# Placing TensorE's side work between attention steps: taking turns, early fetches, and an account of a small lead

## The chip, the cores and the metric

The kernel runs on one core of one Trainium2 chip. The metric is device microseconds (us) of one execution. Before the change it takes 8251.99 us, the median of three runs (8248.94 to 8252.69).

## The reference, cut to what matters

The input x has 4 images of 64 x 64 positions with 128 channels. Each image becomes 4096 tokens of 128 channels.

```python
# layer 0: two 3x3 convolutions, a gate, strictly causal attention with 4-wide queries and keys
c1 = conv_same(elu(x), W1, b1);  a, b = split(conv_same(c1, W2, b2), 2)
c3 = a * sigmoid(b)
q, k, v = c3 @ Wq + bq, c3 @ Wk + bk, c3 @ Wv + bv
x = x + c3 + tile(softmax_masked(q @ k.T / 4) @ v, 8) @ W3 + b3
# layer 1: full attention over 4096 tokens, 16 heads of 8, a gated FFN, 2 of 8 experts
n = layernorm(x)
h = n + concat_heads(softmax(q1 @ k1.T) @ v1) @ wo        # q1, k1, v1 = n @ wq, wk, wv
t = x + h + silu(h @ w1) * (h @ w3) @ w2
y = layernorm(t)
p, i = top_2(softmax(y @ router_w));  p = p / sum(p)
out = t + sum_j p_j * (y @ expert_w[i_j] + expert_b[i_j])
```

## The kernel before, in words

**The main work.** Layer 1's attention is 4096 *steps*: for each image (batch) b, each of 4 groups g of four heads, each of 8 blocks c of 512 queries and each of 32 tiles of 128 keys, one step (`attention_step`, L820) makes four score matmuls into two PSUM buffers `s` of 128 x 1024, two exponentials of 128 x 1024 on ScalarE into `e`, and four value matmuls that add into the one PSUM bank `acc`. There are three buffers `s` (L134), so the scores of a step and a half can stand ready. Layer 0's attention adds 36 such steps for each batch (`first_step`, L745), which put their sums in the bank `m`. In the main loop a step's values are issued after the scores of the second step after it (`finish(2)`, L1267).

**The side work.** Everything else that TensorE does (convolutions in Winograd form, projections, FFN, experts) is written as Python generators that are cut into *pieces*, each of about half a PSUM bank's worth of matmuls. All pieces share the one PSUM bank `m` (`bank`, L162; `m_tile`, L141): a *tile* here is one filling of that bank, made of a first piece, marked "held", and a last piece, marked "stop", and VectorE has to copy it out before the next tile may begin. A piece yields its estimated TensorE time (0.46 us for most, 0.0 for one that issues only VectorE, ScalarE, GpSimd or DMA work).

The generators are, for each batch: `convolutions` (L439), which turns the image into `c3`; `first_attention` (L576), which makes layer 0's queries, keys and values for a block and asks for its first steps; `second_operands` (L650), which makes layer 1's q, k and v of a block and writes them to device memory; and, for each block whose attention is complete, `last_part` (L863): attention output, FFN, router and experts. `last_part` starts by reading four operands from device memory, inverts the softmax sums on VectorE, writes them out and reads them back spread over the channels (`d_r<-sums`, `per<-d_r`).

**The order.** It is written out by hand: `InOrder` (L95) keeps each engine's instructions as the Python code issues them. `run_alone` (L1044) first brings batch 0 to the point where two blocks of second operands exist. Then the main loop (L1243) issues a step, and between the step's scores and an older step's values it may call `insert` (L245), which advances the first filler in the list `fillers` by one piece. It does so while `credit` is positive; `credit` grows each step by a rate that spreads the fillers' remaining estimated time (`PREPARE`, `LAST`, L1231) over the batch's remaining steps. No piece is inserted in a segment's first two steps (`quiet`, L1197). When the next segment's operands are not ready, the loop goes round without a step and inserts a piece each time (`waiting`): here called a *waiting place*.

`plan` (L1146) lets batch 0 begin with 2 blocks of keys (64 steps), go on when 4 exist (192 steps) and finish when all 8 do. Batch 0 thus computes its later blocks while its own attention runs. After `run_alone`, its chain is strictly sequential: `first_attention` calls the convolutions when it lacks `c3`, waits for its first steps, and then runs `second_operands` itself; `second_operands_beside` (L736) ends.

Of the kernel before, what the change touches and what calls it, by code (L numbers as in the profile page):

```python
# [12 lines left out]
ALU = mybir.AluOpType  # L13
# [102 lines left out]
def fast_path(ctx: ExitStack, tc: tile.TileContext, a: dict, where: dict, out: bass.AP, verdict):  # L116
# [122 lines left out]
    def advance(part):  # L239

        r = next(part[0], None)
        part[1] = max(0.5, part[1] - (r[0] if r else 0.0))
        return r

    def insert():  # L245
# [102 lines left out]
    def winograd(u, cols, v, bias, used, final):  # L348

        late = []  # L350
        for q, j in enumerate(COLS):
            sd = chunk("sd")
            s, d = wk.tile([P, QB // 2], FP, tag="sums", bufs=1, name="sums"), sd[:, : QB // 2]
            for pair in ((1, 2), (0, 3)):
                if late:
                    late.pop(0)()
                ps = bank()
                part = [ps[:, : QB // 2], ps[:, QB // 2 :]]
                for m, i in zip(part, pair):
                    product(m, u[:, 4 * i + j, cols], v[q][:, i])  # L360
                    if i == pair[0]:
                        yield 0.46, "held"
                if pair[0] == 1:
                    if alone[0]:
                        act.activation(sd, ps, AF.Copy)
                    else:
                        dve.tensor_copy(sd, ps)
                    dve.tensor_tensor(s, d, sd[:, QB // 2 :], ALU.add)
                    dve.tensor_tensor(d, d, sd[:, QB // 2 :], ALU.subtract)
                else:  # L370
                    t = chunk("neg", "t2")
                    if q == 0:

                        dve.scalar_tensor_tensor(t[:, : QB // 2], part[0], bias, s, ALU.add, ALU.add)
                        dve.scalar_tensor_tensor(t[:, QB // 2 :], d, bias, part[1], ALU.add, ALU.subtract)
                    else:
                        dve.tensor_tensor(t[:, : QB // 2], part[0], s, ALU.add)
                        dve.tensor_tensor(t[:, QB // 2 :], d, part[1], ALU.subtract)
                    used(q)
                    if q == 0:  # L380
                        one = t
                    elif q == 1:
                        both, less = chunk("pos", "both"), chunk("pos", "less")
                        (dve if alone[0] else pool).tensor_tensor(both, one, t, ALU.add)
                        pool.tensor_tensor(less, one, t, ALU.subtract)
                    elif q == 2:
                        late += final(0, t, both, ALU.add)
                    else:
                        late += final(1, less, t, ALU.subtract)
                yield 0.46, "stop"  # L390
        while late:
            yield 0.0, "stop"
            late.pop(0)()

    def first_band(st):

# [42 lines left out]
    def convolutions(b, st):  # L439
# [4 lines left out]
        def elu(n):  # L444

            todo = range(made[0], n)
            made[0] = max(made[0], n)
            neg, pos = {}, {}
            for at in range(len(todo) + 2 if todo else 0):
                a_, b_, c_ = (todo[i] if 0 <= i < len(todo) else None for i in (at, at - 1, at - 2))  # L450
                if b_ is not None:

                    pos[b_] = chunk("pos")
                    dve.tensor_scalar(pos[b_], xs[b_], 0.0, None, ALU.max)
                    dve.scalar_tensor_tensor(pos[b_], neg[b_], 1.0, pos[b_], ALU.min, ALU.add)
                    if b_ + 2 < NQ:
                        xs.append(load_x(b, b_ + 2, "xe"))
                if a_ is not None:
                    neg[a_] = chunk("neg")
                    act.activation(neg[a_], xs[a_], AF.Exp)  # L460
                if c_ is not None:
                    r, k = divmod(c_, 2)
                    ps = bank()
                    transposed(pos[c_], ps)
                    put = [(r, slice(1 + 8 * k, 9 + 8 * k), slice(0, 8))]
                    if k == 0 and r > 0:
                        put.append((r - 1, slice(17, 18), slice(0, 1)))
                    if k == 1 and r < 3:
                        put.append((r + 1, slice(0, 1), slice(7, 8)))
                    for band, to, of in put:  # L470
                        dve.tensor_scalar(
                            e_band[band % 2][:, to, 1 : IMG + 1], rows(ps)[:, of], -1.0, None, ALU.add
                        )
                yield (0.0 if c_ is None else 0.6), "stop"

        def first(r):
            band = c_band[r % 2]
# [50 lines left out]
        for n, (layer, r) in enumerate(jobs):  # L528
# [25 lines left out]
                if r == 3:  # L554
                    pool.memset(here[:, 17, :], 0.0)
            else:
                while alone[0] and len(st.ready) < 2 * r - 2:
# [18 lines left out]
    def first_attention(b, st):  # L576
# [3 lines left out]
        for c in range(NQ):  # L580
            while len(st.done) <= c:

                yield (0.0, "wait") if alone[0] else next(st.conv, (0.0, "stop"))
            while alone[0] and st.second < c - 1:
                yield 0.0, "wait"
            c3 = st.done[c]
            t = xt
# [46 lines left out]
            dve.tensor_tensor(t, ps, t, ALU.add)  # L634
            yield 0.6, "stop"

            while alone[0] and st.read < c:
                yield 0.0, "wait"
            sums, found = [], []
            for r in range(c + 1):  # L640
# [1 line left out]
            while not found:  # L642
                yield 0.0, "rounds"
            st.ready.append((t, found[0]))
            while not alone[0] and st.second <= c:
                yield from second_operands(b, st)
        dve.tensor_reduce(seen[:, 0, b : b + 1], top0.rearrange("p i c -> p (i c)"), AX.X, ALU.max)
        dve.tensor_reduce(seen[:, 1, b : b + 1], top_v0, AX.X, ALU.max)
# [1 line left out]
    def second_operands(b, st):  # L650
# [10 lines left out]
        for pair in range(2):  # L661
# [12 lines left out]
            yield 0.46, "stop"  # L674
        h = chunk("h")
        layernorm(t, h)
        for _ in range(2):
            yield 0.0, "stop"
# [57 lines left out]
    def second_operands_beside(b, st):  # L736

        while st.second < NQ:
            while len(st.ready) <= st.second or not folded[0]:
                if not alone[0]:  # L740
                    return
                yield 0.0, "wait"
            yield from second_operands(b, st)

# [75 lines left out]
    def attention_step(b, seg, kt, place, qx, vg, part):  # L820
# [19 lines left out]
        def values(es):  # L840
# [8 lines left out]
            if kt == seg.hi - 1:  # L849
# [5 lines left out]
                to = scratch[b]["a"][c, g] if seg.hi == NT else scratch[b]["p"][g, c]  # L855
                sp.dma_start(out=to, in_=at)
                if seg.hi == NT and g == NG1 - 1:
                    fillers.append([last_part(b, c), LAST])

        return scores, values  # L860


    def last_part(b, c):  # L863
        d = scratch[b]
        t, h, an = chunk("xt", "t"), chunk("xe", "h"), chunk("pos", "an")

# [4 lines left out]
        sp.dma_start(out=h, in_=d["h"][c])  # L871
        sp.dma_start(out=t, in_=d["t"][c])
        for _ in range(3):
            yield 0.0, "stop"
        dve.reciprocal(rs, rs)
        sp.dma_start(out=d["r"][c], in_=rs)
        per = chunk("pos", "per")
# [1 line left out]
            out=per, in_=d["r"][c].rearrange("(j i) n -> j (i n)", i=HD1).unsqueeze(1).to_broadcast([NH1, HD1, QB])  # L879
        )  # L880
        for _ in range(4):
            yield 0.0, "stop"
        dve.tensor_tensor(an, an, per, ALU.mult)
        yield 0.0, "stop"
        ps = bank()
        tokens(ps, an, wo1, range(2))
        yield 0.46, "held"
# [35 lines left out]
        dve.tensor_tensor(t, ps, t, ALU.add)  # L923
        y = chunk("h", "y2")
        layernorm(t, y)
        yield 0.46, "stop"
        for _ in range(3):
            yield 0.0, "stop"

        ps = bank()  # L930
        transposed(y, ps)
# [32 lines left out]
        yield 0.24, "stop"  # L964
        act.activation(pr, lg, AF.Exp)
        yield 0.0, "stop"
        yield 0.0, "stop"
        m1, w1 = top(pr, "a")
        rest = small("rest", [4, NE])
# [15 lines left out]
        by_block = d["g"][c].rearrange("(b e) (k a) -> b e k a", e=SLOT, a=SLOT)  # L985
        for b_ in range(4):
            sp.dma_start(out=g8.rearrange("e (k b a) -> b e k a", k=4, a=SLOT)[b_], in_=by_block[b_, :NE])
        for _ in range(6):
            yield 0.0, "stop"

        ps = bank()
        tokens(ps, g8, eb, range(2))
        yield 0.46, "held"
        tokens(ps, g8, eb, range(2, 4))
        dve.tensor_tensor(t, ps, t, ALU.add)
        yield 0.46, "stop"
        for k in range(4):
            tk = t[:, k * C : (k + 1) * C]
            by_e = wk.tile([P, NE, C], FP, tag="two", bufs=1, name="by_e")
            for half in range(2):  # L1000
# [8 lines left out]
                if half == 1:  # L1009
                    added = chunk("w", "added")[:, :C]  # L1010
                    dve.tensor_reduce(added, by_e.rearrange("p e c -> p c e"), AX.X, ALU.add)
                    dve.tensor_tensor(tk, tk, added, ALU.add)
                yield 0.46, "stop"
        sp.dma_start(out=tb_o[b][:, 4 * c : 4 * c + 4, :], in_=by_k(t))


# [23 lines left out]
            batches.append(self)  # L1040

    batches = []

    def run_alone(gens, until):  # L1044

# [182 lines left out]
        yield from spread(pool, taps2b, wino2[:, :, C:])  # L1228


    PREPARE, LAST = 149.0, 20.8  # L1231
    st = batches[0]
    left = run_alone(
        [st.conv, first_attention(0, st), second_operands_beside(0, st), fold_and_spread(), spread_beside()],
        lambda: st.second >= plan[0].n and len(spread_of) == 3,
    )
    alone[0] = False

    fillers.extend([gen, PREPARE] for gen in reversed(left[1:]) if gen is not st.conv)

    steps = stream()
    credit, waiting = 0.0, False
    while True:  # L1243
        if steps_in:
            do_step(steps_in.pop(0))
# [9 lines left out]
        b = now[0]  # L1255
        if batches[b].second == NQ and len(batches) == b + 1 and b + 1 < B:
            Batch(b + 1)
            fillers.append([first_attention(b + 1, batches[b + 1]), PREPARE])

        rate = 1.0  # L1260
        if batches[b].second == NQ:
            within = steps_left[b] - 40 if b + 1 < B else min(steps_left[b] - 40, 160)
            rate = sum(us for _, us in fillers) / max(1, within)
        credit = min(0.7, credit + rate)
        if waiting or credit > 0.0 and not quiet[0]:
            credit -= insert()
        finish(2)  # L1267
    finish(0)
    alone[0] = True
# [718 lines left out]
```

## Time and profile before

| | |
|---|---|
| median of 3 runs | 8251.99 us |
| the profiled execution's own time | 8255.66 us |
| its span | 8253.9 us |
| mean granted TensorE clock | 0.983 of full speed |
| TensorE busy | 8031.3 us, 97% |
| ScalarE busy | 7874.2 us, 95% |
| VectorE busy | 2468.4 us, 30% |
| GpSimd busy | 680.1 us, 8% |
| instructions of ScalarE | 8679, of which 8480 are exponentials |

The profile is of one execution, 3.7 us above the median. PE is TensorE, PEld its weight loads, ACT ScalarE, DVE VectorE, POOL GpSimd, SP the engine that issues the DMAs; "L105" stands on every row, because one helper issues every instruction, so rows are told apart by tile names. A TensorE that is shown busy may be computing at half clock, so its busy share says little by itself. ScalarE's records overlap: an exponential's record lasts 1.10 us on average, but the next one begins before it ends. In the view by stages each row is a stretch of time, with each engine's busy time in it, the granted clock and the DMA's share.

### The profile page before, as it was taken

Reading aid. Unit: us, or ns where it says so; the run is one execution under the profiler, and the core shown is the slowest. Engines: PE = TensorE matmul, PEld = TensorE weight load, DVE = VectorE, ACT = ScalarE, POOL = GpSimd, SP = SyncE. Lnnn points to the kernel's source line nnn. Section 1 sums busy time; section 2 is a strip of 40 time slices with the busy share of each in tenths; the row PEclk is TensorE's granted clock in tenths of the full one; section 3 lists DMA queues with packets and bytes.
Section 4 is the critical chain, followed back from the end, with each engine's and each line's share of the span. In section 5 each row is a group of like instructions: output and inputs, shape, how many; then the busy total and the mean of one; then the engine's idle time right before and its main releaser. Section 6 shows DMA issues by size and latency. Waiting matters only on the chain.

```text
span 8253.9 us, 172977 instructions
## 1 busy us (share of the span) xinstructions
PE 8031.3 (97%) x73299; PEld 2481.4 (30%) x73299; DVE 2468.4 (30%) x5068; ACT 7874.2 (95%) x8679; POOL 680.1 (8%) x615
## 2 busy tenths in 40 slices
PE   7799999999999999999999999999999999999997
PEld 3222222223333322333333333233333333332233
DVE  4433222222322223333322222343332222221223
ACT  3599999999999999999999999999999999999996
POOL 2210211000000003110000000311100000000000
PEclk8799999999999999999999999999999999999998
DMA  2121001101100001111100000111111111111211
GB/s 75 52 71 64 27 32 40 52 26 50 48 24 24 30 19 35 35 38 47 39 30 25 27 28 19 33 36 48 35 42 49 44 40 46 52 38 38 66 60 38
DMA packets 213940, 334.24 MB, mean 40 GB/s; under 512 B 31555, under 2 KB 107811, under 8 KB 213155
## 3 DMA queue, kind: packets, MB, share of 16 engines
q1 hardware_dynamic: 209139, 321.31, 11.9%
q8 instruction: 577, 9.45, 0.5%
q10 hardware_dynamic: 4016, 1.77, 0.1%
q14 instruction: 208, 1.70, 0.1%
HBM read 195.09 MB, written 127.93 MB: 39 GB/s over the span
## 4 chain that ended last, share of the span: by engine, by line
PE 87%; issue 7%; DVE 2%; ACT 1%; DMA 1%; POOL 1%; SPq 0%; ACTq 0%; DVEq 0%; POOLq 0%
PE acc L105 42%; PE s L105 29%; PE m L105 17%; ACT e L105 1%; DVE h L105 0%; POOL rs L105 0%; DMA f_kx<-d_k 0%; DVE pos L105 0%; DVE added L105 0%; DMA xe<-in_x_dram 0%; POOL xt L105 0%; DVE at L105 0%; SPq L105 0%; DMA d_r<-sums 0%; DVE two L105 0%
## 5 line engine op out<-in xcount | busy, mean ns | idle before, releaser
L105 ACT ACTIVATE e<-s 128x1024 f32<-128x1024 f32 (+1 forms) x8480 | 7814.2, 1101 | 144.5 <-PE s L105 137.9
L105 PE MATMUL acc<-e,vg 128*9 128x512 f32 x32768 | 4335.4, 595 | 1.0 <-DVE at L105 1.0
L105 PE MATMUL s<-qx,f_kx 32*128 32x512 f32 (+2 forms) x16960 | 2912.0, 496 | 40.3 <-ACT e L105 24.8
L105 PEld LDWEIGHTS s<-qx,f_kx 32*128 32x128 f32 (+1 forms) x16960 | 1165.5, 182 | 4089.1 <-ACT e L105 3872.2
L105 PEld LDWEIGHTS acc<-e,vg 128*9 128x9 f32 x32768 | 719.6, 90 | 798.0 <-issue 458.5
L105 PE MATMUL m<-v,f_wino 128*32 128x256 f32 x5744 | 468.1, 400 | 18.8 <-POOL v L105 7.3
L105 DVE TENSOR_TENSOR by_e<-m,gates 128x512 f32<-128x512 f32 x245 | 169.4, 691 | 681.6 <-PE m L105 681.6
L105 POOL TENSOR_TENSOR v<-r 128x1024 f32<-128x1024 f32 x120 | 232.6, 1945 | 1160.7 <-PE m L105 1160.3
L105 DVE COPY sd<-m 128x512 f32<-128x512 f32 x179 | 123.7, 691 | 633.5 <-PE m L105 633.5
L105 PE MATMUL m<-f_we,y2T 128*32 128x256 f32 x3920 | 313.1, 391 | 0.0
L105 POOL TENSOR_TENSOR rs<-ve,f_minus_half 128x4 f32<-128x4 f32 x64 | 65.3, 1020 | 2843.5 <-DVE ve L105 2819.8
L105 DVE TENSOR_REDUCE added<-by_e 128x128 f32<-128x1024 f32 x128 | 255.7, 1998 | 4.4
L105 DVE TENSOR_TENSOR t<-m,t 128x512 f32<-128x512 f32 x62 | 42.9, 692 | 698.7 <-PE m L105 698.7
L105 POOL TENSOR_TENSOR t<-t,h 128x512 f32<-128x512 f32 x32 | 40.9, 1277 | 2527.4 <-DVE h L105 2527.4
L105 DVE COPY at<-acc 128x512 f32<-128x512 f32 x130 | 89.9, 692 | 521.3 <-PE acc L105 521.3
L105 PE MATMUL m<-hT,f_fw 128*32 128x256 f32 (+1 forms) x2728 | 236.1, 391 | 0.0
L105 DVE TENSOR_TENSOR t<-m,sums 128x256 f32<-128x256 f32 x135 | 57.3, 424 | 480.1 <-PE m L105 480.1
L105 PEld LDWEIGHTS m<-v,f_wino 128*32 128x32 f32 x5744 | 116.4, 109 | 203.5 <-issue 155.0
L105 DVE SCALAR_TENSOR_TENSOR h<-m,h 128x512 f32<-128x512 f32 (+1 forms) x93 | 64.2, 690 | 352.6 <-ACT th L105 254.5
L105 DVE COPY h<-m 128x512 f32<-128x512 f32 (+1 forms) x93 | 64.2, 690 | 314.1 <-PE m L105 314.1
L105 PE MATMUL m<-e,f_v 128*32 128x512 f32 (+2 forms) x1128 | 154.0, 593 | 0.0
L105 DVE TENSOR_TENSOR e<-e,f_consts 128x128 f32<-128x128 f32 x128 | 29.1, 286 | 315.1 <-ACT e L105 315.1
(253 smaller groups left out, 3319.9 us busy)
## 6 DMA issues: line engine op xcount, KB each, us to landing
f_kx<-d_k SPq DMA_DIRECT2D x139, 512.0 KB
qx<-d_q SPq DMA_DIRECT2D x152, 256.0 KB
d_q<-two SPq DMA_DIRECT2D x64, 512.0 KB
d_a<-at SPq DMA_DIRECT2D x128, 256.0 KB
vg<-d_v SPq DMA_DIRECT2D x32, 576.0 KB
d_k<-two SPq DMA_DIRECT2D x32, 512.0 KB
d_v<-vc SPq DMA_DIRECT2D x32, 288.0 KB
xe<-in_x_dram SPq DMA_DIRECT2D x32, 256.0 KB
```

The lines of the kernel that those rows point to most:

```text
L105: made = op(*args, **kw)
```

## The change

The change touches the order of issue only; the matmuls, exponentials and transfers are the same, but for one zero-time piece.

1. **Turns.** What `run_alone` leaves of batch 0 (convolutions, first attention, second operands) becomes one filler, `together`, which goes round the three generators a piece at a time, finishing a tile once begun. Until four blocks of second operands exist (`plan[0].n + 2`), two pieces are inserted at a place in place of one. Tests of `alone[0]` inside the generators become tests of `b == 0`.
2. **Early fetch.** The first part of `last_part` (the reads, the reciprocal, `d_r`, `per`, the product) becomes `operands`, advanced by one part after each expert tile of the block before, if a later block is waiting. The product with the experts' bias (`tokens(ps, g8, eb)`) moves from before the experts to after them, and the six empty places that stood before it go.
3. **Account.** A piece is placed only when TensorE's lead, counted by four constants, covers it, or when credit is above 2.8. Places with no TensorE work, now marked "free", may be taken without credit. Credit may grow to 3.0 in place of 0.7; PREPARE is 143.3 in place of 149.0, LAST 18.9 in place of 20.8.

```diff
@@ advance @@
         part[1] = max(0.5, part[1] - (r[0] if r else 0.0))
+        part[3] = r is not None and r[1] in ("free", "rounds")
         return r
@@ first_attention @@
-                yield (0.0, "wait") if alone[0] else next(st.conv, (0.0, "stop"))
-            while alone[0] and st.second < c - 1:
+                r = (0.0, "wait") if b == 0 else next(st.conv)
+                if r[1] != "done":
+                    yield r
+            while b == 0 and st.second < c - 1:
                 yield 0.0, "wait"
...
-            while not alone[0] and st.second <= c:
+            while b > 0 and st.second <= c:
                 yield from second_operands(b, st)
@@ second_operands_beside @@
-                if not alone[0]:
-                    return
                 yield 0.0, "wait"
@@ last_part, its head split off @@
+    def fetch(b, c):
+        if (b, c) not in fetching:
+            fetching[b, c] = operands(b, c)
+        return next(fetching[b, c], fetching) is None
+
+    def fetch_following(b, c):
+        keys = [part[2] for part in fillers]
+        at = keys.index((b, c)) + 1
+        if at < len(keys) and keys[at]:
+            fetch(*keys[at])
+
+    def last_part(b, c):
+        d = scratch[b]
+        while fetch(b, c):
+            yield 0.0, "free"
+        t, h, an = fetched.pop((b, c))
...
-        for _ in range(6):
-            yield 0.0, "stop"
-        ps = bank()
-        tokens(ps, g8, eb, range(2))
...
         for k in range(4):
...
+                fetch_following(b, c)
                 yield 0.46, "stop"
@@ new @@
+    def together(gens):
+        gens = list(gens)
+        while gens:
+            for _ in range(len(gens)):
+                r = next(gens[0], None)
+                while r is not None and r[1] in ("held", "rounds"):
+                    yield r
+                    r = next(gens[0], None)
+                gen = gens.pop(0)
+                if r is not None:
+                    gens.append(gen)
+                    if r[0] > 0.0:
+                        yield r[0], "stop"
+                        break
+                if not gens:
+                    return
+            else:
+                yield 0.0, "stop"
@@ the main loop @@
-    PREPARE, LAST = 149.0, 20.8
+    PREPARE, LAST = 143.3, 18.9
...
-    fillers.extend([gen, PREPARE] for gen in reversed(left[1:]) if gen is not st.conv)
+    fillers.append([together(left), PREPARE, None, False])
+    EXPS, SCORES, VALUES, PIECE, AHEAD = 1.81, 0.43, 0.987, 0.446, 0.18
+    ahead = 0.0
...
-        credit = min(0.7, credit + rate)
-        if waiting or credit > 0.0 and not quiet[0]:
-            credit -= insert()
+        credit = min(3.0, credit + rate)
+        left = ahead + EXPS - SCORES - (VALUES if len(undone) > 2 else 0.0)
+        free = bool(fillers) and fillers[0][3]
+        if waiting or not quiet[0] and (free or credit > 0.0 and (left >= PIECE or credit > 2.8)):
+            took = insert()
+            if b == 0 and batches[0].second < plan[0].n + 2:
+                took += insert()
+            credit -= took
+            left -= took
+        ahead = min(max(left, 0.0), AHEAD)
         finish(2)
```

More of the change, by code (lines that the diff above doesn't have):

```diff
@@ L389, in winograd @@
                         late += final(1, less, t, ALU.subtract)
-                yield 0.46, "stop"
+                yield 0.46, "free" if q == 3 and pair[0] == 0 and late else "stop"
         while late:
-            yield 0.0, "stop"
             late.pop(0)()
+            yield 0.0, "free" if late else "stop"
     def first_band(st):
@@ L473, in elu @@
                         )
-                yield (0.0 if c_ is None else 0.6), "stop"
+                yield (0.0 if c_ is None else 0.6), "free" if at == 0 else "stop"
         def first(r):
@@ L556, in convolutions @@
             else:
-                while alone[0] and len(st.ready) < 2 * r - 2:
+                while b == 0 and len(st.ready) < 2 * r - 2:
                     yield 0.0, "wait"
@@ L635, in first_attention @@
             yield 0.6, "stop"
-            while alone[0] and st.read < c:
+            while b == 0 and st.read < c:
                 yield 0.0, "wait"
@@ L673, in second_operands @@
                 st.read += 1
-            yield 0.46, "stop"
+            yield 0.46, "free" if pair == 1 else "stop"
         h = chunk("h")
@@ L677, in second_operands @@
         for _ in range(2):
-            yield 0.0, "stop"
+            yield 0.0, "free"
         sp.dma_start(out=d["t"][c], in_=t)
@@ L857, in values, with operands @@
                 if seg.hi == NT and g == NG1 - 1:
-                    fillers.append([last_part(b, c), LAST])
+                    fillers.append([last_part(b, c), LAST, (b, c), False])
         return scores, values
-    def last_part(b, c):
+    fetching, fetched = {}, {}
+    def operands(b, c):
         d = scratch[b]
@@ L873, in last_part @@
         for _ in range(3):
-            yield 0.0, "stop"
+            yield
         dve.reciprocal(rs, rs)
@@ L881, in last_part @@
         for _ in range(4):
-            yield 0.0, "stop"
+            yield
         dve.tensor_tensor(an, an, per, ALU.mult)
-        yield 0.0, "stop"
+        fetched[b, c] = t, h, an
+        yield
+    def fetch(b, c):
[10 more added lines that the diff above has]
+        while fetch(b, c):
+            yield 0.0, "free"
+        t, h, an = fetched.pop((b, c))
         ps = bank()
@@ L925, in last_part @@
         layernorm(t, y)
-        yield 0.46, "stop"
-        for _ in range(3):
-            yield 0.0, "stop"
+        yield 0.46, "free"
+        for i in range(2):
+            yield 0.0, "free" if i == 0 else "stop"
         ps = bank()
@@ L963, in last_part @@
         pr = small("pr", [4, NE])
-        yield 0.24, "stop"
+        yield 0.24, "free"
         act.activation(pr, lg, AF.Exp)
-        yield 0.0, "stop"
+        yield 0.0, "free"
         yield 0.0, "stop"
@@ L987, in last_part @@
             sp.dma_start(out=g8.rearrange("e (k b a) -> b e k a", k=4, a=SLOT)[b_], in_=by_block[b_, :NE])
-        for _ in range(6):
-            yield 0.0, "stop"
-        ps = bank()
-        tokens(ps, g8, eb, range(2))
[L993 to L996, printed above, removed]
         for k in range(4):
@@ L1012, in last_part @@
                     dve.tensor_tensor(tk, tk, added, ALU.add)
+                fetch_following(b, c)
                 yield 0.46, "stop"
+        ps = bank()
+        tokens(ps, g8, eb, range(2))
+        yield 0.46, "held"
+        tokens(ps, g8, eb, range(2, 4))
+        dve.tensor_tensor(t, ps, t, ALU.add)
+        yield 0.46, "stop"
         sp.dma_start(out=tb_o[b][:, 4 * c : 4 * c + 4, :], in_=by_k(t))
@@ L1257, in fast_path @@
             Batch(b + 1)
-            fillers.append([first_attention(b + 1, batches[b + 1]), PREPARE])
+            fillers.append([first_attention(b + 1, batches[b + 1]), PREPARE, None, False])
         rate = 1.0
@@ L1262, in fast_path @@
             within = steps_left[b] - 40 if b + 1 < B else min(steps_left[b] - 40, 160)
-            rate = sum(us for _, us in fillers) / max(1, within)
-        credit = min(0.7, credit + rate)
-        if waiting or credit > 0.0 and not quiet[0]:
-            credit -= insert()
+            rate = sum(part[1] for part in fillers) / max(1, within)
+        credit = min(3.0, credit + rate)
[8 more added lines that the diff above has]
+        ahead = min(max(left, 0.0), AHEAD)
         finish(2)
```

## The prediction, made before the changed kernel ran

> **What bounds the kernel now.** I read the page's busy times first, then the view by stages, then the chain of waits in the stage that stands out. The first says that two engines are nearly full, and gives the exponentials:
>
> ```profile
> PE 8031.3 (97%) x73299; PEld 2481.4 (30%) x73299; DVE 2468.4 (30%) x5068; ACT 7874.2 (95%) x8679; POOL 680.1 (8%) x615
> L105 ACT ACTIVATE e<-s 128x1024 f32<-128x1024 f32 (+1 forms) x8480 | 7814.2, 1101 | 144.5 <-PE s L105 137.9
> ```
>
> ScalarE is idle for 8253.9 - 7874.2 = 379.7 us; nearly all its work is fixed. The view by stages tells where those 379.7 us are (columns: stretch, length, busy PE, PEld, DVE, ACT, POOL with counts, granted clock, DMA share, GB/s):
>
> ```profile
> 0.00:150.00 150.00, 92.92 (x336) 47.24 (x336) 80.50 (x164) 15.57 (x22) 44.28 (x65) 0.84 0.29 84
> 150.00:273.00 123.00, 122.03 (x1144) 36.45 (x1144) 42.52 (x73) 118.54 (x129) 34.59 (x27) 0.95 0.15 44
> 273.00:385.00 112.00, 69.85 (x568) 25.59 (x564) 57.74 (x130) 20.85 (x25) 16.07 (x14) 0.56 0.19 65
> 385.00:780.00 395.00, 380.71 (x3514) 115.91 (x3506) 135.61 (x302) 378.86 (x416) 44.09 (x36) 0.98 0.17 56
> 780.00:820.00 40.00, 23.91 (x204) 9.24 (x202) 15.84 (x35) 21.83 (x25) 4.03 (x6) 0.75 0.50 163
> 850.00:8165.00 7315.00, 7273.83 (x67156) 2211.77 (x67148) 2087.63 (x4268) 7283.44 (x8024) 520.20 (x455) 1.00 0.12 38
> 8165.00:8254.00 89.00, 38.65 (x191) 27.11 (x183) 42.59 (x85) 6.94 (x10) 2.42 (x3) 0.66 0.08 24
> ```
>
> Length minus ACT: 134.4 us of ScalarE's idling lie before 150, 4.5 in the first 64 steps, 91.2 in the wait for four blocks of operands, 16.1 and 18.2 behind it, 31.6 in the 7315 us from 850 on, 82.1 in the tail. So the steady part is ScalarE's: 7315 us leave 31.6. Records overlap, which hides small slips: undisturbed exponentials follow each other at about 0.915 us (ACT's timeline at 7214 and 7235 has rows of 14 in 12.94 us and 26 in 24.04; less the last record's 1.10, that is 0.911 and 0.918), so that stage's 7857 exponentials and 167 short operations of some 0.4 us need about 7260, and the true slack is some 55 us. TensorE's 97% there is not its limit: a step without a piece needs 0.43 us of scores and 0.99 of values, one with a 0.45 us piece 1.87, against 2 x 0.915 = 1.83 on ScalarE.
>
> The wait at 273 to 385 is a chain, one tile after another:
>
> ```profile
> 275.25 1.11 PE m L105 x16
> 276.38 0.76 DVE t L105 x2
> 277.15 0.14 issue
> 277.28 1.89 PE m L105 x16
> 279.20 0.70 DVE sd L105
> 279.90 0.04 issue
> 279.94 1.98 PE m L105 x16
> ```
>
> TensorE fills bank m, VectorE empties it (0.70 or 0.76), TensorE begins again: 2.7 us a tile. A tile takes 0.92 us in the stream and 1.9 here, because the clock is halved. The ten microseconds that follow show it (clock column 0.50):
>
> ```profile
> 280.00:290.00 10.00, 5.75 (x48) 1.81 (x48) 7.75 (x11) 0.63 (x1) 5.01 (x4) 0.50 0.00 0
> ```
>
> [...] TensorE was not idle between 280 and 290 but 58% busy, and stayed halved. [...] where GpSimd's row terms meet a normalisation: four writes of h take 4.82 us here, of y in the tail 1.11.
>
> ```profile
> 1289.31 4.82 DVE L105 TENSOR_SCALAR h<-xt,mv,rs 128x128 f32<-128x128 f32 x4 [1.14 <-POOL rs L105]
> 1289.33 4.72 POOL L105 TENSOR_TENSOR r<-f_c_band 128x528 f32<-128x528 f32 x4
> ```
>
> **Part 1, the tail: -15 us.** After the last step the last block's `last_part` runs alone. Before, block 6's last expert tiles still stand ahead of it:
>
> ```profile
> 8176.20 1.88 DVE added L105
> 8178.91 2.31 DMA sums<-d_a
> 8220.68 2.23 DMA d_g<-turned
> 8227.23 5.76 PE s L105 x16
> ```
>
> In the changed order of issue block 6 is done some 26 steps before the end. The read `sums<-d_a` then waits only for the write of d_a, issued at 8171.72; writes in the chain take 2.6 us (d_r, 32 KB) to 3.4 (d_k, 512 KB), so it starts near 8174.7: -4.2. The gates are ready on VectorE at 8220.66. Before, the experts stood behind d_g, its four reads (to 8227.1) and the bias product; their first `by_e` came at 8231.31 and their last at about 8246. Now TensorE starts them after the router, and VectorE's four rounds of 1.28 + 1.90 + 0.29 = 3.47 run from 8220.7 to 8234.6, then the bias product's addition 0.7: t is ready at 8235.5 instead of 8246.3, -10.8. The d_g trip (6.5 us) hides under those 14 us; without that cover it would cost what it does today.
>
> **Part 2, batch 0: +12 us.** I counted its places in both orders up to step 72.
>
> *First wait and steps 1 to 18.* Four tiles instead of two before the first scores, which waited for the keys' DMA until 149.53: two further tiles, at 2.7 from 145.2, pass that by some 3.4; with a cold start, +4. Then 17 steps (11 here, 6 later) carry both halves of a tile: 1.42 + 0.92 = 2.34 against 1.83, 8.7 us, less what the places without pieces give back: +7.
>
> *Steps where two tiles meet.* In 21 steps the two pieces are the end of one tile and the start of another, so that TensorE stands still inside the step until VectorE has emptied m: 0.8 to 1.0 us in the rows "PE m <- DVE sd, t" at 273 to 290. Queued behind that piece are the older step's values and the next scores, and ScalarE waits for those. A step takes 0.43 + 0.46 + 0.9 + 0.46 + 0.99 = 3.24, 1.41 over ScalarE's 1.83: 21 x 1.41 = +29. From below it costs 21 x 0.5 = 11, if the emptying were hidden; from above see the slower rival. For a few half-clock windows [...] I add 4: +33.
>
> *The wait itself.* Before, it has 62 waiting places from 273.7 to 374.6: 101 us, of which the first steps of blocks 2 and 3 with cold matmuls take 10.3 + 12.7. After, the first steps and both blocks' layer 0 queries lie in the stream, and 28 places with 28 tiles remain. The two chains of second operands cost, from the trace, 10.4 (block 2 from its transposition on) and 18.0 - 4.5 of waiting for h = 13.5. But turns also put 18 convolution tiles between them: 18 x 2.84 = 51. With values to finish (2.6), the end of the keys' write and read (3.6) and a wait for GpSimd's terms between convolution jobs (6.6 at 402) that is 88. ScalarE's idling falls from 91 to 85: -6.
>
> *After it.* All eight blocks are ready at step 234; before, at step 289, where the stream stood: the stage 780 to 820 loses its 18.2. The 402 us wait has moved into the wait just counted: -8. Sum 4 + 7 + 33 - 6 - 18 - 8 = +12.
>
> **Part 3, steady part: -8 us.** After 850 the account breaks runs of steps with a piece: in batch 1, 198 of 285 runs have two; before, runs of three and more hold 60% of the pieces. A piece costs ScalarE 1.87 - 1.83 = 0.04 at most, some 1200 steps stand in longer runs: 48 at most, of which the 55 us of slack show that not all is lost. Its larger slips (1 to 3 us: h against GpSimd, `neg` waiting for the first read of an image) are ordered as before. I take -8, between -31.6 (all idling) and +8 (a few more half-clock windows). The early fetches put the DVE waits for `sums` and `per` (82 and 215 us in all) out of the way; ScalarE kept going through them, so they earn nothing. Their DMAs only move on SP's queue, where the next reads stand steps ahead of use; a read stuck behind d_a's write holds it 3 us.
>
> **Sum.** -15 + 12 - 8 = -11. The profiled execution took 8255.66, 3.7 above the median; -11 on it is 8244.7, and on the median 8252.0 it is **8241**. A measurement of this kernel can tell about 0.2% (16.5 us) from no change; 8241 is within it.
>
> **Rivals.** *Slower:* TensorE's clock. In the 21 steps TensorE idles 0.9 of 3.24 us. For it: 42% idling kept the clock halved at 280. Against: only 28% here, and two unbroken steps follow at each segment's start. At half clock such a step takes 0.80 + 0.97 + 0.9 + 0.97 + 1.93 = 5.57, 2.33 more: all 21 give +49, 8290. It is slower than no change beyond 0.2% from (16.5 + 11)/2.33 = 12 steps on. 0.24.
>
> *Faster:* the convolution tiles fit into the gaps of the second operands' chains and the emptying hides, 28 tiles x 0.9 = 25 less in the wait, and the account finds 12 more: 8204. For it: the chains stand still 5.5 and 4.5 us for h. Against: one bank m. 0.36, with all that ends below 8235.5.
>
> *Not as said:* the account changes nothing, because TensorE never was late: 8249, within the same band.
>
> **How the numbers follow.** No change within 0.2% is likeliest at 0.40, with 8236 to 8268 its own range; faster 0.36, slower 0.24. The range, 8200 to 8285, reaches from the faster case nearly to the slower one.
>
> **What would show it.** ScalarE idle near 45 us more than now in the first 75 steps; a wait of about 88 us with clock 0.5 behind step 71; no gap near step 289; `by_e` of the tail starting before g8 is read. A clock of 0.5 through the first 70 steps makes the slower rival right; a wait under 60 us, or under 20 us of ScalarE idling after 850, the faster one.

## The result, and the profile after

The changed kernel takes **8229.71 us**, the median of 11 runs (8223.49 to 8233.66), against 8252.12 for the kernel before, 11 runs on the same chip (8248.13 to 8257.38). The ratio is 0.9973, 95% interval 0.9965 to 0.9981: 22.4 us or 0.27% faster. The prediction was 8241, with a range of 8200 to 8285.

The page of the changed kernel, its busy times first and its exponentials second:

```profile
PE 8022.1 (97%) x73335; PEld 2481.8 (30%) x73335; DVE 2459.5 (30%) x5068; ACT 7866.6 (96%) x8679; POOL 681.1 (8%) x615
L105 ACT ACTIVATE e<-s 128x1024 f32<-128x1024 f32 x8480 | 7809.3, 1112 | 91.5 <-PE s L105 87.1
```

The work is unchanged. ScalarE's idling is 8228.1 - 7866.6 = 361.5 us where it was 379.7. But the exponentials' records overlap: they last 1.112 us on average, and the 14 in the row of 13.00 us shown under account_undone begin (13.00 - 1.11)/13 = 0.915 apart. That hides small slips in the busy times, so I count from here on by the end of a step's second exponential. The view by stages of the changed kernel, cut where its own stages begin (columns as before: stretch, length, busy PE, PEld, DVE, ACT, POOL, granted clock, DMA share, GB/s):

```profile
150.00:326.00 176.00, 152.18 (x1499) 48.95 (x1500) 79.93 (x165) 134.49 (x145) 49.37 (x38) 0.98 0.11 34
326.00:415.00 89.00, 51.62 (x474) 19.99 (x470) 50.35 (x94) 2.91 (x5) 31.22 (x25) 0.55 0.23 79
415.00:780.00 365.00, 349.96 (x3104) 106.54 (x3104) 129.98 (x294) 347.79 (x384) 35.38 (x31) 0.97 0.23 74
780.00:850.00 70.00, 69.56 (x600) 20.59 (x600) 17.72 (x32) 70.00 (x79) 15.02 (x11) 1.00 0.16 49
850.00:8160.00 7310.00, 7274.48 (x67206) 2216.41 (x67196) 2068.14 (x4246) 7293.53 (x8045) 503.06 (x443) 1.00 0.12 38
8160.00:8229.00 69.00, 29.74 (x123) 21.74 (x119) 32.77 (x74) 2.31 (x5) 2.42 (x3) 0.71 0.09 26
```

The stretch with steps 1 to 71 now leaves ScalarE 41 us idle (176 - 134.49) at a clock of 0.98, then comes one wait of 89 us at a clock of 0.55, the stand near 800 is gone (70.00 of 70), and the tail is 69 us long. The next table counts from the exponentials in the traces, in us. Step 1 is the first step of the main loop; three steps of layer 0 lie before it, so that the last step is 4237.

| kernel | end of step 72 | steps 73 to 300 | steps 301 to 4237 | tail | span |
|---|---|---|---|---|---|
| before | 377.4 | 461.5 | 7330.9 | 84.1 | 8253.9 |
| changed | 414.8 | 440.6 | 7304.8 | 67.9 | 8228.1 |
| difference | +37.4 | -20.9 | -26.1 | -16.2 | -25.8 |
| predicted | +38 | -26 | -8 | -15 | -11 |

Batch 0 (the first two columns) and the tail came as worked out. The steady part gave three times as much.

The same columns for the experiments' profiled executions:

| kernel | end of step 72 | 73 to 300 | 301 to 4237 | tail | median, us |
|---|---|---|---|---|---|
| turns_undone | 373.4 | 449.2 | 7310.8 | 68.4 | 8201.1 |
| turns_single | 433.0 | 438.1 | 7307.2 | 68.7 | 8251.0 |
| turns_whole_tiles | 400.6 | 439.5 | 7308.7 | 68.0 | 8216.9 |
| chain_whole_tiles | 346.1 | 451.5 | 7308.6 | 68.3 | 8175.6 |
| whole_tiles_alone | 341.3 | 461.4 | 7332.8 | 84.6 | 8221.8 |
| account_undone | 417.2 | 438.3 | 7313.3 | 67.7 | 8242.6 |
| fetch_undone | 416.9 | 438.3 | 7309.9 | 67.8 | 8233.4 |
| bias_first | 414.5 | 437.1 | 7367.7 | 77.6 | 8298.6 |
| bias_first_no_fetch | 414.8 | 437.3 | 7326.0 | 117.9 | 8295.6 |
| bias_first_sooner | 415.0 | 440.7 | 7314.5 | 78.3 | 8249.5 |
| bias_alone | 369.1 | 461.1 | 7325.5 | 68.3 | 8226.2 |
| account_alone | 372.2 | 450.0 | 7321.8 | 117.7 | 8271.2 |

Two cautions. The kernel before and bias_alone issue the same instructions in the same order up to step 72, yet end it at 377.4 and 369.1. Up to 8 us in the first column say nothing by themselves. The medians were taken in several sessions, in which the kernel before took 8252.1, 8252.1, 8254.3 and 8254.4; where two kernels come from different sessions, some 2 us say nothing either.

### The profile page after: what moved, and what is told of

It reads as the page before. It is cut to its first block, busy times and chain, and to the rows that moved or that the text cites. A ratio compares the mean times of both kernels' runs of the same rounds, so it can differ in the third digit from the quotient of the medians.

```text
span 8228.1 us, 173041 instructions
## 1 busy us (share of the span) xinstructions
PE 8022.1 (97%) x73335; PEld 2481.8 (30%) x73335; DVE 2459.5 (30%) x5068; ACT 7866.6 (96%) x8679; POOL 681.1 (8%) x615
## 4 chain that ended last, share of the span: by engine, by line
PE 67%; issue 3%; ACT 1%; DVE 1%; POOL 0%; DMA 0%; ACTq 0%; DVEq 0%; POOLq 0%
PE acc L105 33%; PE s L105 22%; PE m L105 13%; ACT e L105 1%; DVE h L105 0%; POOL rs L105 0%; DVE added L105 0%; DVE at L105 0%; ACT neg L105 0%; POOL xt L105 0%; ACT t L105 0%; DVE by_e L105 0%; POOL v L105 0%; ACT th L105 0%; DMA d_r<-sums 0%
## 5 line engine op out<-in xcount | busy, mean ns | idle before, releaser
L105 ACT ACTIVATE e<-s 128x1024 f32<-128x1024 f32 x8480 | 7809.3, 1112 | 91.5 <-PE s L105 87.1
L105 PE MATMUL s<-qx,f_kx 32*128 32x512 f32 (+1 forms) x16960 | 2909.2, 495 | 37.5 <-ACT e L105 27.7
```

Of the source, the lines that this page charges most:

```text
L105: made = op(*args, **kw)
```

## Experiments on batch 0: what the turns cost

**turns_undone.** The changed kernel with batch 0's sequential chain put back, one piece at a place.

```diff
-                while b == 0 and len(st.ready) < 2 * r - 2:
+                while alone[0] and len(st.ready) < 2 * r - 2:
...
-    fillers.append([together(left), PREPARE, None, False])
+    fillers.extend([gen, PREPARE, None, False] for gen in reversed(left[1:]) if gen is not st.conv)
...
-            if b == 0 and batches[0].second < plan[0].n + 2:
-                took += insert()
```

> The changed kernel with batch 0's chain sequential again and one piece a place; account, fetches and the moved bias product stay. Theory (turns lose in the first 75 steps what the later stall pays back, net 16 us by step 300): about 8214 us, step 72 near 377 us in its profile as in the kernel before. Rival (turns are what made the change faster, the account nothing): 8245 or more.

Measured: 8201.1 (8196.25 to 8203.52), ratio to before 0.9937 (0.9923 to 0.9951), 28.6 us under the changed kernel. The turns with their two pieces are a loss: 41.4 us at step 72, of which 8.6 come back by step 300. The kernel is 13 us faster than expected: the turns cost more than the 16 us that I had charged them with here. In part that is because the chain put back doesn't repeat the kernel before: step 290, where the stream stands, takes 11.2 us, and 21.9 in the kernel before. The account does that (11.8 us in account_alone below, which has no turns).

**turns_single.** Turns kept, one piece at a place.

```diff
-            if b == 0 and batches[0].second < plan[0].n + 2:
-                took += insert()
```

> The changed kernel with turns but one piece a place. Theory (the doubling bought about as much wait as it cost in the stream): the stream to step 64 ends near 273 as in the kernel before, then 95 waiting places at 1.4 us; step 72 at 405 to 425, 8222 to 8240. Rival (the doubling was the loss): step 72 near 380, 8195 to 8205.

Measured: 8251.0 (8244.24 to 8255.38), ratio 0.9998 (0.999 to 1.0007). Both expectations missed: the second piece is a gain of some 20 us (21 in the medians, 19 in the traces). Without it the steps up to 71 run undisturbed, but the stream stands at steps 65 (37.3 us) and 68 (25.6 us) for layer 0's operands of blocks 2 and 3, and the wait at 72 is 91.8 us all the same. Doubling costs ScalarE 41 us in those steps and saves both stands, 59 us. The loss lies in the turns.

**turns_whole_tiles and chain_whole_tiles.** A second piece is taken only if the first began a tile, so that no step holds the end of one tile and the start of another; once with turns, once with the chain of turns_undone.

```diff
+        begun[0] = r is not None and r[1] == "held"
...
-            if b == 0 and batches[0].second < plan[0].n + 2:
+            if b == 0 and batches[0].second < plan[0].n + 2 and begun[0]:
                 took += insert()
```

> The changed kernel, but the second piece of a place is taken only where it completes the tile that the first began; turns stay. Theory (two tiles that meet inside a step cost 0.9 us each, 21 times): step 72 ends some 19 us earlier than in the changed kernel (395 for 414.8), about 8211. Rival (the loss of the first 75 steps is the wait at half clock, or the doubled matmuls themselves): step 72 stays within 5 us of 415, 8225 to 8235.

> Batch 0's chain sequential as in turns_undone (8201 us, step 72 at 373.4), with whole tiles in a step until four blocks are ready. Theory (a tile in the stream costs ScalarE 0.51 us, in the wait 2.7; the turns lost because convolution tiles stood in the wait): 24 further tiles go into the stream for 12 us, the wait of 101 us shrinks to some 45: step 72 near 335, about 8163. Rival (what is taken out of the wait comes back as stalls in the stream): step 72 at 365 or later, 8190 to 8205.

Measured: 8216.9 (8213.06 to 8218.55), ratio 0.9955 (0.9941 to 0.9969), and 8175.6 (8173.74 to 8176.46), ratio 0.9906 (0.989 to 0.9921). The second misses its 8163 by 12 us and its step 72 by 11. The first is 12.8 us under the changed kernel, close to its 8211. Its steps 5 to 71 lose 24.2 us over 1.83 each where the changed kernel loses 40.8, and none takes 3.0 to 3.8 us; in the changed kernel 18 do. One of these in the changed kernel's timeline (start, length, engine, operation, in brackets the idling before it; rows that don't bear on the reading, weight loads among them, are left out here and below):

```profile
271.80 0.51 PE L105 MATMUL s<-qx,f_kx 32*128 32x512 f32 x4
272.24 0.66 PE L105 MATMUL m<-f_consts,c 128*128 128x128 f32 x4
...
273.00 0.69 DVE L105 TENSOR_TENSOR xt<-m,xt 128x512 f32<-128x512 f32 x1 [1.05 <-PE m L105]
273.75 0.64 PE L105 MATMUL m<-v,f_wino 128*32 128x256 f32 x8 [0.85 <-DVE xt L105]
...
275.77 6.52 ACT L105 ACTIVATE e<-s 128x1024 f32<-128x1024 f32 x7 [1.44 <-PE s L105]
```

A tile ends at 272.9, VectorE empties m, TensorE stands 0.85 us until the next tile may begin, values and scores queue behind it, and ScalarE idles 1.44. From 271.80 to the next scores at 275.17 the step takes 3.37 us.

Whole tiles with the chain are the best version of this study, 79 us under the kernel before of the same session and 54 under the changed kernel. The two kernels of this pair differ only in the order in which batch 0's tiles come, and that is worth 41 us. The view by stages of chain_whole_tiles shows where:

```profile
150.00:285.00 135.00, 129.31 (x1262) 42.64 (x1262) 66.57 (x129) 118.76 (x129) 46.02 (x36) 0.97 0.14 44
285.00:346.00 61.00, 41.01 (x375) 15.46 (x373) 32.78 (x72) 17.05 (x19) 2.19 (x3) 0.66 0.32 110
```

ScalarE idles 16 us in the first stretch and 44 in the waits, against 41 and 86 in the changed kernel. With turns, the convolutions of later blocks take places ahead of the second operands of blocks 2 and 3, which alone release the stream, and then do so in the wait, at a mean clock of 0.55. The convolutions' matmuls alone (tile `f_wino`, 16 to a tile) in the wait of the changed kernel, then in that of chain_whole_tiles:

```profile
326.00:415.00 89.00, 33.94 (x288) 0.55 0.23 79
312.10:346.10 34.00, 6.15 (x52) 0.55 0.34 118
```

That is 18 tiles against 3. Two of the 18 in the changed kernel's timeline:

```profile
368.58 1.94 PE L105 MATMUL m<-v,f_wino 128*32 128x256 f32 x16 [1.22 <-DVE xt L105]
370.65 0.42 DVE L105 TENSOR_TENSOR t<-m,sums 128x256 f32<-128x256 f32 x1 [2.21 <-PE m L105]
...
371.55 1.93 PE L105 MATMUL m<-v,f_wino 128*32 128x256 f32 x16 [1.03 <-DVE t L105]
```

Each takes 1.9 us, and they begin 3.0 apart, while ScalarE stands. With turns and whole tiles there are again 288 such matmuls, 18 tiles, in a wait of 91.8 us, and the chain's wait is 34.1. Fifteen tiles at 3.0 us are 45 of these 58 us; the rest is not attributed.

**whole_tiles_alone.** The same rule in the kernel before, and nothing else.

```diff
+        begun[0] = r is not None and r[1] == "held"
...
         if waiting or credit > 0.0 and not quiet[0]:
             credit -= insert()
+            if b == 0 and batches[0].second < plan[0].n + 2 and begun[0]:
+                credit -= insert()
```

> The kernel before with nothing but two pieces at a place, and these only where both belong to one tile, until four blocks of second operands exist. Theory: what a whole tile in a step costs (some 0.5 us of ScalarE) is less than what a tile costs in the wait at half clock (some 2.7 us), whatever else is in the kernel; it took 27 us off step 72 in the sequential chain with the account. Near 8225. Rival: without the account the stream's first steps come late already, and the wait takes its time from the reads and writes in its chain: 8240 to 8252.

Measured: 8221.8 (8217.58 to 8224.43), ratio 0.9961 (0.9947 to 0.9974). As the theory said; the rest of the table row is within 2 us of that of before. These few lines do about as much as the whole change (the two intervals overlap).

## Experiments on the steady part and the tail

**account_undone.**

```diff
-        credit = min(3.0, credit + rate)
+        credit = min(0.7, credit + rate)
...
-        if waiting or not quiet[0] and (free or credit > 0.0 and (left >= PIECE or credit > 2.8)):
+        if waiting or credit > 0.0 and not quiet[0]:
```

The constants PREPARE and LAST stay as changed.

> The changed kernel with the old rule for placing a piece (credit up to 0.7, a piece whenever credit is positive). Theory (the account spaces the three transpositions at each image's start and thins runs of pieces, which saved 18 us or more behind step 300): slower than the changed kernel by 15 to 22 us, 8245 to 8252, with the slips of 1 to 3 us at the image starts back. Rival (the steady gain came from the early fetches): 8228 to 8233.

Measured: 8242.6 (8236.75 to 8245.68, 21 runs), ratio 0.9987 (0.998 to 0.9994). The account is worth 12.9 us here, less than the 15 to 22 expected and more than the rival's nothing. The profiled execution is 4.2 us under this median; its span is 8.5 us longer than the changed kernel's, and so are its steps 301 to 4237. About 6 of the 8.5 lie at the image starts, where the old rule issues transpositions of elu(x) in neighbouring places. The same two transpositions for the third image in three timelines, first before, then account_undone, then the changed kernel (from 5037 to 5052 us):

```profile
5205.24 1.08 PE L105 MATMUL m<-f_consts,pos 128*128 128x128 f32 x4 [1.11 <-DVE f_e_band L105]
...
5208.98 1.94 ACT L105 ACTIVATE e<-s 128x1024 f32<-128x1024 f32 x2 [2.81 <-PE s L105]
```

```profile
5053.28 1.09 PE L105 MATMUL m<-f_consts,pos 128*128 128x128 f32 x4 [2.45 <-DVE f_e_band L105]
...
5057.02 1.94 ACT L105 ACTIVATE e<-s 128x1024 f32<-128x1024 f32 x2 [4.00 <-PE s L105]
```

```profile
5039.91 13.00 ACT L105 ACTIVATE e<-s 128x1024 f32<-128x1024 f32 x14
...
5043.31 0.66 PE L105 MATMUL m<-f_consts,pos 128*128 128x128 f32 x4
```

Before, the second transposition waits 1.11 us for the first to be copied out, and ScalarE idles 2.81; with the old rule in the changed kernel it waits 2.45, and ScalarE idles 4.00. In the changed kernel the account leaves a place empty between them, and the exponentials go through. I call a step a slip when it takes over 1 us more than 1.83. After 850, before has 12 slips (26.6 us in all), the changed kernel 5 (11.7), and account_undone only 6 (14.7): most of before's slips are gone without the account's rule, too.

**fetch_undone.** The line `fetch_following(b, c)` is left out.

> The changed kernel without the early fetch; each block fetches its operands at its own start. Theory (VectorE's waits for the operands cost nothing): 8226 to 8234, the same. Rival (the early fetches made the steady part faster): 8240 to 8250.

Measured: 8233.4 (8227.83 to 8235.41), ratio 0.9978 (0.9969 to 0.9987): 3.7 us, as the theory said, and hardly to be told from nothing.

**bias_first.** The experts' bias product and its six empty places are put back ahead of the experts, and the product behind them goes.

```diff
+        for _ in range(6):
+            yield 0.0, "stop"
+        ps = bank()
+        tokens(ps, g8, eb, range(2))
+        yield 0.46, "held"
...
         for k in range(4):
...
-        ps = bank()
-        tokens(ps, g8, eb, range(2))
-        yield 0.46, "held"
...
```

> The changed kernel with the bias product ahead of the experts and its six empty places back. Theory (in the tail the experts stand behind the gates' trip again): slower by about 11 us, 8241, all of it after the last step. Rival (the trip was hidden anyway): 8230.

Measured: 8298.6 (8296.53 to 8304.79), ratio 1.006 (1.0046 to 1.0074). The tail is 9.7 us longer, near the 11 expected, but steps 301 to 4237, which were to stay as they were, take 62.9 us more: 25 slips of over 1 us, 67.4 us in all, against 5 and 11.7 in the changed kernel. One of them in its timeline:

```profile
6400.60 0.29 DVE L105 TENSOR_TENSOR t<-t,added 128x128 f32<-128x128 f32 x1
6400.81 0.68 DVE L105 TENSOR_TENSOR an<-an,per 128x512 f32<-128x512 f32 x1
...
6401.65 0.64 PE L105 MATMUL m<-f_wo,an 128*32 128x128 f32 x16 [2.49 <-DVE an L105]
...
6403.68 3.77 ACT L105 ACTIVATE e<-s 128x1024 f32<-128x1024 f32 x4 [2.49 <-PE s L105]
```

The next block's product `an` is issued with the last expert tile, so VectorE reaches it only after by_e, added and t; the next block's first matmul follows in the next place and waits 2.49 us. In the changed kernel the bias product stands between them.

**bias_first_no_fetch.** bias_first without `fetch_following(b, c)`.

> The kernel bias_first (8298.6 us) without the early fetch. Theory (in bias_first the product of the fetched operands stands on VectorE behind the last expert tile's reduction, with no piece between, and the first matmul of the next block waits for it 2.5 us, 24 times): without the fetch those slips go, 8240 to 8250, of which about 11 in the tail. Rival (the bias product's own wait for the gates' trip is the stall): 8290 to 8300 as before.

Measured: 8295.6 (8293.84 to 8299.96), ratio 1.0052 (1.0039 to 1.0066). The total is the rival's, the trace is not. The slips fell to 12 (28.4 us), and steps 301 to 4237 to 7326.0, 41.7 less than in bias_first. But the tail grew by 40.3, as the view by stages shows:

```profile
8178.00:8296.00 118.00, 48.54 (x206) 36.84 (x201) 57.09 (x129) 2.81 (x7) 3.56 (x5) 0.65 0.06 18
```

Block 6 of the last image is still in its FFN when the stream ends: its router, gates and experts then precede the last block's fetch, whose read of the sums starts only at 8221.83, 43.8 us after the last exponential. Without the fetch a block needs more empty places, and the account refuses others: account_alone below, without early fetch too, has the same tail, the kernel before, without the account, 84.1. Two causes of one size made one total.

**bias_first_sooner.** To separate them without a place more: bias_first, with the fetch going two parts on at the first expert tile, so that `an` is issued with the seventh.

```diff
                 fetch_following(b, c)
+                if k == 0 and half == 0:
+                    fetch_following(b, c)
```

> The kernel with the bias product ahead of the experts, whose fetch of the next block goes two parts on at the first expert tile, so that the product an*per is issued with the seventh expert tile in place of the eighth. No place is added. Theory: the 24 slips of some 2.5 us came from the first matmul of the next block standing directly behind that product, which VectorE reaches only after by_e, added and t. One tile earlier they are gone: 40 us less than with the product in the eighth tile, near 8257. Rival: the slips come from the bias product ahead of the experts, with its wait for the gates' trip through device memory: 8290 to 8300 as before.

Measured: 8249.5 (8246.49 to 8251.52), ratio 0.9994 (0.9986 to 1.0002), 49 us under bias_first and 7 under the theory's figure; 8 slips over 1 us are left of 25. So the position of `an` was the cause, and the bias product ahead of the experts with its six places costs what is left, 7314.5 - 7304.8 = 9.7 us in the steps and 10.4 in the tail.

**bias_alone.** The kernel before, with the bias product moved behind the experts and the six places dropped.

> Part open: steps 300 to 4237 take 26 us less in the changed kernel than in the one before, and the account (8.5 us) and the fetch (5) explain only half. This kernel is the one before with nothing but the experts' bias product moved behind the experts, its six empty places dropped. Theory: the move pays in the stream too, since each of 31 blocks needs six places less; without fetch, steps 300 to 4237 took 7326.0 us with the bias product ahead of the experts and 7309.9 with it behind, 16 us. Steps 300 to 4237 then take 7315 us in place of 7331, the tail loses 10 as in the changed kernel: near 8227. Rival: the move is worth its tail alone, and the 16 us came from late placing under the account: 8241.

Measured: 8226.2 (8222.22 to 8227.77), ratio 0.9966 (0.9954 to 0.9978). The total is that of the theory, its parts only half: steps 301 to 4237 gain 5.4 us, not 16, and the tail 15.8, not 10 (block 6 is done some 23 steps before the end). The other 8 us lie ahead of step 72, where the order is that of before; I don't count them for the move, and why they are there stays open. So this move alone, like the whole tiles alone, gives as much as the whole change: what the turns lose, 28.6 us by turns_undone, uses up what the other parts gain.

**account_alone.** The kernel before with the account alone; built from turns_undone with bias product and fetch as before.

> The kernel before with nothing but the account: no turns, no early fetch, bias product ahead of the experts. Theory: the account refuses places, and with six empty places for each block the blocks no longer fit. Batch 0 gains as in the kernel without turns (-16 at step 300), steps 300 to 4237 gain about 5 (7326 against 7331), but block 6 of the last image is not done when the stream ends, and the tail takes about 118 us in place of 84: near 8265. Rival: the account alone is what makes the stream smooth, steps 300 to 4237 lose 20 us, and the tail stays at 84 to 90: near 8220.

Measured: 8271.2 (8263.46 to 8276.55, 14 runs), ratio 1.0022 (1.0014 to 1.003). The tail is 117.7, as the theory said, and steps 301 to 4237 gain 9.1 us where it said 5: without the places that the other parts free, the account is a loss. The profiled execution is the fastest of the 14, 7.7 us under the median, so the trace leaves that much unexplained.

## Why the prediction was right, and where it was wrong

**Tail, -15 against -16.2: right, by its mechanism.** The changed kernel's chain of waits, then its timeline:

```profile
8162.05 2.01 DMA d_a<-at
...
8164.07 2.10 DMA sums<-d_a
```

```profile
8205.70 1.25 DVE L105 TENSOR_TENSOR by_e<-s,gates 128x512 f32<-128x512 f32 x2
...
8207.39 2.87 SPq L105 DMA_DIRECT2D g<-d_g  x4
...
8214.81 1.15 PE L105 MATMUL s<-f_eb,g 8*128 8x128 f32 x8
```

The read of the sums starts as d_a's write has landed, with no experts of block 6 ahead; by_e starts before the gates' reads are issued, and the bias product of 1.15 us runs while VectorE still works on the experts' sums. Block 6 is done 28 steps before the end, where 26 were counted. The tail of bias_first, 77.6 us, splits the 16.2 into 6.5 for what stood ahead and 9.7 for the experts, against 4.2 and 10.8.

**Steps where two tiles meet, 21 of 3.24 us: right.** 20 steps take 3 us or more, 18 of them 3.38 on average; the loss in steps 5 to 71 is 40.8 us against 7 + 33. Of the 33, 4 were an estimate of mine for half-clock windows, whose length I had from no trace; from 154.6 us to the wait this trace has a single one, 3.41 us at 0.51. The slower rival needed a halved clock in 12 of them; the stage has 0.98. The faster one needed the wait under 60 us. The +37.4 of the whole first column is near +38, but only within the 8 us of the first caution above.

**The wait, 88 us: right.** It is 88.7 from step 71 to 72, at a clock of 0.50 from 335.5 us on. The 51 us charged to convolution tiles were the right suspicion: with whole tiles, the sequential order saves 41 us.

**After it, -26 against -20.9: nearly.** The stand at step 290 (289 in the prediction's count) is gone, 21.9 us, and so are those at 86 and 120, 10.8 and 6.6. Three new ones of 5 to 7 us, at steps 131, 159 and 236, were not foreseen.

**Steady part, -8 against -26.1: the term that was mis-sized.** It measured three times its size, inside the bound of -31.6. Two statements in it failed. "Larger slips ... are ordered as before": they were not; slips over 1 us fell from 26.6 us to 11.7. At the image starts the account spaces the transpositions; in all the account gives 8.5. That the early fetches "earn nothing" was nearly so (5.1 in the trace, 3.7 in the medians). And the moved bias product was priced in the tail only: with its six empty places, which no run separates from it, it is worth 9.7 us in the steps (5.4 in the kernel before, 16.1 without the fetch). These three make 23.3 of the 26.1. They were measured by undoing one part each and need not add up, and the change's other small moves of empty places, in the convolutions and ahead of the router, were never undone by themselves.

**The call.** "Within 0.2%" was named likeliest, and the result is 0.27% faster. It lies in the case given 0.36, though not by that case's mechanism: the steady part paid, not the wait. That the total came inside a range 85 us wide says little; the table of parts says more.

## What to carry to other kernels

Before interleaving chains, ask which one releases the stalled engine: giving turns to the others put 18 tiles among its own in the wait, at a mean clock of 0.55. When two pieces go into one place, let them be the two halves of one tile; here a place in which one tile ended and another began paid for the copy between them, 0.85 us of TensorE standing and 1.44 of ScalarE in the step shown. Empty places of a schedule are a resource, and when one is removed or an early product added, look at what is now neighbour to what: `an` directly ahead of its matmul cost 49 us, and two variants with equal totals lost them in different stages.

## What the runs showed of the hardware

In the changed kernel TensorE's granted clock was 1.00 from 154.6 to 294.5 us, with TensorE busy for 119.64 of 139.90 us and 18 pauses of 0.7 to 1.5 us in it, most of them in the steps where two tiles meet. After one longer pause, 1.91 us at 292.67, it was 0.51 for 3.41 us. In the wait it was 0.50 from 335.5 us on, with TensorE busy 47.84 of 79.5 us, or 60%. It rose at 420.8 us, after TensorE had been busy for 8.56 of 8.8 us. In the kernel before it was 0.50 from 150 to 155 us, with TensorE shown busy for 4.85 of the 5 us. What makes the clock fall or rise, these runs don't settle.
